# A PixArt block on one core: setup in single words and a new prelude order, gate-bias products on GpSimd, tokens in pairs, the query's cut ahead of the norms

## The chip, the cores and the metric

The kernel runs on one core of a Trainium2 chip. A core has four compute engines with instruction streams of their own: TensorE (PE; its weight loads are a second row, PEld), VectorE (DVE), ScalarE (ACT) and GpSimd (POOL). SyncE (SP) here only issues DMAs; ACT and POOL issue a few as well. The metric is the device time of one execution in microseconds (us); lower is better.

## The reference

A diffusion-transformer block over x of 16 batches x 256 tokens x 256 features, in float32, with 16 heads of 16 and a context of 256 tokens for each batch:

```
c_proj = silu(c) @ W_mod + b_mod          # shift_a, scale_a, gate_a, shift_m, scale_m, gate_m
x_norm = ln(x) * (1 + scale_a) + shift_a
q, k, v = split(x_norm @ W_qkv + b_qkv)
x = x + gate_a * (softmax(q k^T / 4) v @ W_proj + b_proj)
q_c = ln(x) @ W_qc + b_qc;  k_c, v_c = split(ln(context) @ W_kvc + b_kvc)
x = x + softmax(q_c k_c^T / 4) v_c @ W_cproj + b_cproj
x_norm2 = ln(x) * (1 + scale_m) + shift_m
x = x + gate_m * (gelu(x_norm2 @ W_mlp1 + b_mlp1) @ W_mlp2 + b_mlp2)
```

## The kernel before

Each operand of the large products is cut into a high and a low part of a reduced 32-bit type (`...h`, `...l` in tile names), and three products, high x high, high x low, low x high, make up one.

*Units.* An attention of one batch is a unit. There are 32: self-attention units s0 to s4, then s5 c0 s6 c1 ... s15 c10, then the cross-attentions c11 to c15. The MLP of all batches follows (the last 220 us of the span). A unit goes through eight beats. In each beat TensorE does the scores of the next unit (row maxima: score tiles `s` and `st`, maxima `mx` on DVE), the second scores `t` and exponentials of the current one, and pieces of what later units need. The table PLAN gives, for each of the eight beats, the words done ahead, the words of two lanes of TensorE (the two halves of the array's rows) and the words done after. `beat` turns each word into calls; units up to four ahead are being prepared while unit n runs.

*Order.* `InOrder` (L40-53) keeps every engine's instructions in the order in which the Python program issues them. So the words decide what stands behind what on each engine. All instructions carry line L51 in the profile, that helper's; they are told apart by tile names.

*Norms and cuts.* `layernorm` (L286) has three steps: the statistics on DVE, `rstd` (DVE aggregates, POOL adds epsilon and takes the power -0.5 in `rs`), and `apply`, on POOL in steady state (tile `xn_s` for x, `xn_c` for the context, `xn_q` for the cross-attention's query). `transposed` (L354) then turns xn on TensorE into `psT_...`, evacuates on ACT (`y_q`) and cuts on POOL: a copy to the high part (`xTh_q`), a subtraction for the low part (`xTl_q`). The query product `ps_qc` reads both. In PLAN's beat 6 the words `s6` and `e6` do rstd and apply of a unit four ahead; beat 7 ends in `Uc`, the cut of the query's transposed input of a unit three ahead.

*Keys and queries.* `to_stack` makes K and Q of a unit: product, high part on ACT (`h_k`, `h_q`), low part on DVE (`l_k`, `l_q`), and six DMAs of 128 KB for each of the two (`send`; words x, y for the high part, l for the low part, each 0 and 1) into a stacked buffer `big`, from which the scores are multiplied. A unit's first score matmul needs all twelve sends of its buffer.

*Prelude.* The string 'PRE' in `E_` (L55) is a list of words done in order before the first beat; 'SL' gives words done after beat k of unit n, as (n, k); n = -1 stands for the eight beats in which only unit 0's first scores run. `b12`, `b4` and so on are fillers: so many matmuls of a zero tile `wz` (`busy`, L155). `load` issues the loads of x of batch 0 (on ACT), the bias rows `brow` and the first weights. `brow` turns the bias rows into `bT`, `turn` turns silu(c) into `sT`, `scale` and `shift` are the two modulation products (both into `cpT`; `sc1` adds one to the scale, tile `sc`), `bk`, `bq`, `bv` are the bias products of the shift with the weights, `hik`/`lok` the cut of a weight (`hiv`/`lov` that of V, its low part on DVE). L, T, K, Q, V with a unit's number are norm, transposition, key, query and value: `L0a`, `L0b` statistics and rstd, `L0d` apply on DVE, `T0t` transposition, `T0h`/`T0l` high and low part; `K0a`, `K0m` the two halves of the key product, `K0h`, `K0l` its parts, `K0x0` ... `K0l1` its sends (with p: issued by POOL). `z0kp` zeroes a buffer on POOL, `M0` transposes maxima, `wm` loads the second modulation's weights, `ld3` loads a unit's input.

*The rest of the setup.* `setup_rest` (L211) is a generator; each word `rest` runs its next piece: the loads, then the attention's gate (`ps_ga`), the projected bias (`ps_pb`) and its product with the gate on DVE, then the cross-attention's bias (`ps_cb`), three weight loads and five cuts of weights. `f_gm` (L268) does the same for the MLP's gate: `ps_gm`, an addition and the product `gB` x gate, both on DVE, and a store to `gd`, from which each batch's gates are later read back.

Of the kernel before, what the change touches and what calls it, by code (L numbers as in the profile page):

```python
# [21 lines left out]
def pixart_block(  # L22
# [8 lines left out]
    B, N, H = x.shape  # L31
# [4 lines left out]
    KC = H // P  # L36
# [58 lines left out]
    BMOD, BQKV, BQC, BKVC, BM1 = 0, 12, 18, 20, 24  # L95
# [40 lines left out]
    st = psum.tile([P, 2, 512], F32, tag="st", name="st", bufs=1)  # L136
    sp = [psum.tile([P, 512], F32, tag=f"s{r}", name=f"s{r}", bufs=1) for r in range(2)]
# [73 lines left out]
    def setup_rest():  # L211
        gb = work.tile([B, 2, 2, H], F32, tag="pt", name="gb", bufs=5)
        gA, bb = gb[:, 0], gb[:, 1]
        bc = const.tile([1, H], F32, name="bc")
        wg, wp = stage(W_mod, 2 * H, "wga", "g", 3), stage(W_proj, 0, "wp_f", "g", 3)
        SP.dma_start(bb[:, 0], b_mod[2 * H:3 * H].partition_broadcast(B))
        SP.dma_start(bb[:, 1], b_proj.partition_broadcast(B))
        SP.dma_start(bc, b_cproj.partition_broadcast(1))
        wcp = stage(W_cproj, 0, "wcp_f", "x1", 7)
        yield  # L220
        pst = ps_gen("ps_ga")
        for k in range(KC):
            PE.matmul(pst[:B, :H], sT[:, k], wg[:, k], start=(k == 0), stop=(k == KC - 1))
        DVE.tensor_tensor(gA[:, 0], pst[:B, :H], bb[:, 0], ALU.add)
        yield
        pst = ps_gen("ps_pb")
        for k in range(KC):
            PE.matmul(pst[:B, :H], bqkv[:, 4 + k], wp[:, k], start=(k == 0), stop=(k == KC - 1))
# [3 lines left out]
        yield  # L232
        pst = ps_gen("ps_cb")
        for k in range(KC):
            PE.matmul(pst[:1, :H], bT[:, BKVC + 2 + k:BKVC + 3 + k], wcp[:, k],
                      start=(k == 0), stop=(k == KC - 1))
        DVE.tensor_tensor(bc, pst[:1, :H], bc, ALU.add)
        SP.dma_start(cd, bc)
        yield
        wkc, wqc = stage(W_kvc, 0, "wkc_f", "g", 3), stage(W_qc, 0, "wqc_f", "c", 2)  # L240
        wvc = stage(W_kvc, H, "wvc_f", "x1", 7)
        yield
        split(Wp[0], Wp[1], wp)
        yield
        split(Wkc[0], Wkc[1], wkc)
        yield
        split(Wqc[0], Wqc[1], wqc)
        yield
        split(Wvc[0], Wvc[1], wvc)
        yield  # L250
        split(Wcp[0], Wcp[1], wcp)

    wm = []

# [8 lines left out]
    gm = []  # L266

    def f_gm():  # L268
        w, gB = gm
        pst = ps_gen("ps_gm")  # L270
        for k in range(KC):
            PE.matmul(pst[:B, :H], sT[:, k], w[:, k], start=(k == 0), stop=(k == KC - 1))
        DVE.tensor_tensor(gB[:, 0], pst[:B, :H], gB[:, 0], ALU.add)
        DVE.tensor_tensor(gB[:, 1], gB[:, 1], gB[:, 0], ALU.mult)
        SP.dma_start(gd[:, 2:4], gB)

    def f_mods():
# [673 lines left out]
        build_pre(u)  # L951
        build_post(u)
    at = defaultdict(list)
    rest = setup_rest()

    u0, u1 = units[:2]
    def one_rows(i):
# [3 lines left out]
    u2 = units[2]  # L961
    word = {}
# [45 lines left out]
    word["rest"] = lambda: next(rest, None)  # L1008
    word["vone"] = lambda: [POOL.memset(v[:, :, :, HD:], 1.0) for v in vts]
    for n, f in (("load", f_load), ("silu", f_silu), ("turn", f_turn), ("brow", f_brow),  # L1010
                 ("scale", f_scale), ("sc1", f_sc1), ("shift", f_shift),
                 ("wm", f_wm), ("mods", f_mods), ("sc2", f_sc2), ("gm", f_gm)):
        word[n] = f
    for i in range(3):
# [8 lines left out]
    for i in range(3):  # L1023
        b = i if i < 2 else 0
# [26 lines left out]
    def visit(n, k, home=sp):  # L1051
# [22 lines left out]
    ]  # L1074
    lanes = {}

    def beat(n, k):
        if n < 0:
            s, t = visit(n, k, (st, sp)[k % 2])
# [19 lines left out]
        def attention(v, hf):  # L1099
# [4 lines left out]
        on = lambda v, f: f if v else lambda: None  # L1104
        T1 = lx and (lx.T[1],)
# [60 lines left out]
        s, t = visit(n, k, home)  # L1166
# [15 lines left out]
    last, o, q = units[-1], units[-1].post, units[-2].post  # L1182
# [86 lines left out]
```

## Time and profile before

| | us |
|---|---|
| median of 3 runs | 747.45 |
| lowest and highest of them | 747.15, 747.74 |
| profiled execution, its own time | 747.02 |
| its span, first to last instruction | 745.2 |

The clock granted to TensorE was 0.999 of full speed in the mean. A row of the timeline reads: start in us from the span's start, duration in us, engine, line, operation, tile written <- tiles read, partitions x elements and type of each, how many instructions the row stands for, and in brackets how long the engine had stood idle and whose end released it. PEld rows are weight loads, one for each matmul, overlapped with the matmul before. SPq, ACTq and POOLq rows are DMA issues. A row of instruction groups has three durations: least, median and largest in ns. A row of the windows view gives a stretch, its length, and for PE, PEld, DVE, ACT and POOL the busy time with the number of instructions, then the clock, the DMA engines' busy share and GB/s.

### The profile page before, as it was taken

Reading aid. Unit: us, or ns where it says so; the run is one execution under the profiler, and the core shown is the slowest. Engines: PE = TensorE matmul, PEld = TensorE weight load, DVE = VectorE, ACT = ScalarE, POOL = GpSimd, SP = SyncE. Lnnn points to the kernel's source line nnn. Section 1 sums busy time; section 2 is a strip of 40 time slices with the busy share of each in tenths; the row PEclk is TensorE's granted clock in tenths of the full one; section 3 lists DMA queues with packets and bytes.
Section 4 is the critical chain, followed back from the end, with each engine's and each line's share of the span. In section 5 each row is a group of like instructions: output and inputs, shape, how many; then the busy total and the mean of one; then the engine's idle time right before and its main releaser. Section 6 shows DMA issues by size and latency. Waiting matters only on the chain.

```text
span 745.2 us, 25296 instructions
## 1 busy us (share of the span) xinstructions
PE 736.1 (99%) x10144; PEld 649.2 (87%) x10144; DVE 575.2 (77%) x1188; ACT 564.1 (76%) x979; POOL 538.3 (72%) x569
## 2 busy tenths in 40 slices
PE   9999999999999999999999999999999999999997
PEld 8778888888888888888888888888879999999997
DVE  4888888888888888888888888888726656667662
ACT  4268898888888888888888887898886666666663
POOL 6757688869687696968769798798647666666652
PEclk9999999999999999999999999999999999999999
DMA  6754454543545445354545445455212132131320
GB/s 203 203 146 138 126 142 136 138 128 91 159 122 139 135 137 143 92 164 120 143 131 152 145 129 159 121 151 151 62 58 91 60 78 67 63 86 43 85 55 32
DMA packets 89049, 87.98 MB, mean 118 GB/s; under 512 B 8610, under 2 KB 84676, under 8 KB 88932
## 3 DMA queue, kind: packets, MB, share of 16 engines
q1 hardware_dynamic: 88468, 85.58, 40.8%
q8 instruction: 80, 1.31, 0.8%
q0 software_dynamic: 192, 0.52, 0.3%
q14 instruction: 37, 0.30, 0.1%
q10 hardware_dynamic: 272, 0.26, 0.1%
HBM read 26.97 MB, written 8.46 MB: 48 GB/s over the span
## 4 chain that ended last, share of the span: by engine, by line
PE 92%; POOL 4%; DVE 1%; issue 1%; DMA 1%; ACT 1%; POOLq 0%; DVEq 0%; ACTq 0%
PE s L51 17%; PE st L51 16%; PE o L51 15%; PE ph L51 11%; PE ps_qc L51 5%; PE ps_q L51 4%; PE ps_kc L51 3%; PE ps_P_s L51 3%; PE ps_k L51 3%; PE ps_v_c L51 3%; PE ps_v_s L51 2%; PE ps_P_c L51 2%; PE psT_q L51 1%; PE psA_s L51 1%; PE ps_h L51 1%; PE psT_m L51 1%
## 5 line engine op out<-in xcount | busy, mean ns | idle before, releaser
L51 DVE TENSOR_REDUCE mx<-s 128x2 f32<-128x512 f32 x504 | 324.6, 683 | 67.2 <-PE s L51 60.4
L51 ACT ACTIVATE pt<-st 128x1024 f32<-128x1024 f32 x252 | 258.9, 1027 | 17.0 <-PE st L51 11.6
L51 PE MATMUL s<-big 63*128 63x256 f32 (+1 forms) x1024 | 182.9, 297 | 0.7 <-DVE mx L51 0.6
L51 PEld LDWEIGHTS s<-big 63*128 63x128 f32 (+1 forms) x1024 | 132.8, 185 | 19.3 <-DVE l_kc L51 6.6
L51 PE MATMUL st<-big 64*128 64x256 f32 (+1 forms) x1024 | 134.1, 299 | 0.3 <-ACT pt L51 0.2
L51 POOL TENSOR_TENSOR hl<-hf,hh 128x512 fp32r<-128x512 f32 x64 | 84.7, 1326 | 64.8 <-ACT hh L51 64.7
L51 PE MATMUL o<-pt,v 128*32 128x256 f32 x2048 | 123.8, 382 | 0.0
L51 PEld LDWEIGHTS st<-big 64*128 64x128 f32 (+1 forms) x1024 | 95.3, 185 | 16.5 <-issue 12.9
L51 PEld LDWEIGHTS o<-pt,v 128*32 128x32 f32 x2048 | 60.0, 109 | 41.4
L51 ACT ACTIVATE hf<-ph,bT 128x256 f32<-128x256 f32 x114 | 47.8, 473 | 27.6 <-PE ph L51 27.6
L51 ACT ACTIVATE hh<-ph,bT 128x256 fp32r<-128x256 f32 x114 | 47.8, 471 | 22.5 <-PE st L51 11.8
L51 ACT COPY oT<-o 128x512 f32<-128x512 f32 x63 | 36.9, 586 | 33.0 <-PE o L51 33.0
L51 DVE TENSOR_SCALAR xn_m<-x,mv_m,rs_m 128x256 f32<-128x256 f32 x28 | 24.0, 901 | 32.4 <-POOL rs_m L51 32.4
L51 PE MATMUL s<-big,hh 128*128 128x256 f32 x256 | 46.7, 281 | 0.0
L51 PE MATMUL st<-big,hh 128*128 128x256 f32 x256 | 46.7, 281 | 0.0
L51 PE MATMUL ph<-wkch,wself 128*128 128x256 f32 x224 | 44.9, 284 | 0.0
L51 PE MATMUL ph<-wqch,wself 128*128 128x256 f32 x224 | 44.7, 284 | 0.0
L51 PE MATMUL ps_k<-xTh_s,wself 64*128 64x256 f32 (+1 forms) x232 | 43.9, 295 | 0.0
L51 PE MATMUL ps_q<-xTh_s,wself 64*128 64x256 f32 (+1 forms) x240 | 39.8, 283 | 0.4 <-DVE l_q L51 0.4
L51 POOL TENSOR_SCALAR xn_c<-c,mv_c,rs_c 128x256 f32<-128x256 f32 x32 | 39.0, 1227 | 1.7
L51 PE MATMUL ps_v_s<-wself,xTh_s 64*128 64x256 f32 x224 | 39.1, 294 | 0.0
L51 PE MATMUL ps_P_s<-wself,xTh_as 64*128 64x256 f32 x256 | 39.0, 282 | 0.0
(244 smaller groups left out, 2519.5 us busy)
## 6 DMA issues: line engine op xcount, KB each, us to landing
big<-h_kc SPq DMA_DIRECT2D x64, 128.0 KB
big<-h_qc SPq DMA_DIRECT2D x64, 128.0 KB
big<-h_k SPq DMA_DIRECT2D x62, 128.0 KB
big<-h_q SPq DMA_DIRECT2D x62, 128.0 KB
big<-l_k SPq DMA_DIRECT2D x32, 128.0 KB
big<-l_q SPq DMA_DIRECT2D x32, 128.0 KB
g<-gd SPq DMA_DIRECT2D x16, 256.0 KB
c<-in_ctx_dram SPq DMA_DIRECT2D x16, 256.0 KB
```

Source lines behind the costliest of these rows:

```text
L51: i = f(*a, **k)
```

## The change

`setup_rest` is split into single words: `lg`, `lp`, `lc`, `lx` for the loads, `ga`, `pb`, `cb` for the three products, `gs` for the product of gate and bias with the store, `sp0` to `sp4` for the cuts. The two products of gate and bias go from DVE to POOL. The tokens of x, context, the spill and the output are laid on partitions in pairs, so each partition holds 2 KB in one piece where it had two of 1 KB. `s6`/`e6` keep rstd alone; a new `s7`/`e7` after `Uc` does apply. PRE and SL have a new order, with other numbers of fillers:

```diff
-'PRE': 'z0qp z0kp load rest ld2 one0 silu b12 brow L0a turn L0b b4 L0d scale T0t sc1 hik lok L1a T0h L1b T0l b4 shift hiq K0a L1d bk loq K0m K0h K0x0 K0x1 K0y0p K0y1p T1t K0l T1h K0l0 K0l1 bq T1l Q0a Q0m Q0h Q0x0 Q0y0p Q0x1 Q0y1p Q0l Q0l0 Q0l1 z1kp z1qp K1a K1b hiv lov Q1a Q1b K1x0 K1x1 K1y0 K1y1 K1l K1l0 K1l1 Q1x0 Q1x1 Q1y0 Q1y1 Q1l Q1l0 Q1l1 L2a L2b L2c V0a V0b bv b9 ld3',
-'SL': {(-1, 0): 'V1a', (-1, 1): 'T2t T2h T2p vone z2kp z2qp', (-1, 2): 'V1b', (-1, 3): 'rest wm', (-1, 4): 'M0 rest one1 ld4', (-1, 5): 'K2a L3a', (-1, 6): 'K2m L3b L3p L3c', (-1, 7): 'mods sc2 one2 rest', (0, 0): 'gm rest', (0, 1): 'rest', (0, 4): 'rest', (0, 6): 'rest', (1, 0): 'rest', (1, 5): 'rest'}
+'PRE': 'b1 b4 load z0kp silu z0qp brow L0a L0b turn scale hik hiq ld2 sc1 L0d T0t T0h lok b3 loq shift T0l L1a L1b L2a hiv lg Q0a bk K0a lp one0 K0m bq lc L1d K0h K0y0p K0x1 Q0m K0l T1t K0l1 Q0h T1h lov T1l bv K1a K1b K0x0 K0y1p z1qp Q0y0p V0a Q1a Q0l Q0x0 K0l0 Q1b Q0l0 z1kp Q0l1 Q0y1p L2b V0b Q0x1 wm Q1l K1y0 Q1x1 K1l b6 ld3',
+'SL': {(-1, 0): 'Q1x0 L2c K1x0', (-1, 1): 'T2t K1l0 V1a T2h vone Q1l1 T2p', (-1, 2): 'V1b', (-1, 3): 'Q1y0 Q1y1 K1y1 pb K1x1 Q1l0 z2kp', (-1, 4): 'one1 L3a z2qp K1l1 ga', (-1, 5): 'K2a L3b K2m', (-1, 6): 'M0 gs', (-1, 7): 'ld4 mods L3p gm', (0, 0): 'L3c lx cb', (0, 4): 'one2', (0, 5): 'sp0', (0, 7): 'sp3 sc2 sp1', (1, 2): 'sp2', (1, 3): 'sp4'}
...
     def tok(ap, b):
-        return ap[b].rearrange("(t p) h -> p t h", p=P)
+        return ap[b].rearrange("(p t) h -> p t h", p=P)
...
+    def f_ga():
         pst = ps_gen("ps_ga")
         for k in range(KC):
-            PE.matmul(pst[:B, :H], sT[:, k], wg[:, k], start=(k == 0), stop=(k == KC - 1))
-        DVE.tensor_tensor(gA[:, 0], pst[:B, :H], bb[:, 0], ALU.add)
-        yield
+            PE.matmul(pst[:B, :H], sT[:, k], gA[2][:, k], start=(k == 0), stop=(k == KC - 1))
+        DVE.tensor_tensor(gA[0][:, 0], pst[:B, :H], gA[1][:, 0], ALU.add)
...
-        DVE.tensor_tensor(gA[:, 1], pst[:B, :H], bb[:, 1], ALU.add)
-        DVE.tensor_tensor(gA[:, 1], gA[:, 1], gA[:, 0], ALU.mult)
-        SP.dma_start(gd[:, 0:2], gA)
-        yield
+        DVE.tensor_tensor(gA[0][:, 1], pst[:B, :H], gA[1][:, 1], ALU.add)
+
+    def f_gs():
+        POOL.tensor_tensor(gA[0][:, 1], gA[0][:, 1], gA[0][:, 0], ALU.mult)
+        SP.dma_start(gd[:, 0:2], gA[0])
...
         DVE.tensor_tensor(gB[:, 0], pst[:B, :H], gB[:, 0], ALU.add)
-        DVE.tensor_tensor(gB[:, 1], gB[:, 1], gB[:, 0], ALU.mult)
+        POOL.tensor_tensor(gB[:, 1], gB[:, 1], gB[:, 0], ALU.mult)
         SP.dma_start(gd[:, 2:4], gB)
...
-        ("", "s t P12", "K2 t s K1 K9", "E n0 Uc"),
+        ("", "s t P12", "K2 t s K1 K9", "E n0 Uc s7 e7"),
...
-            "s6": on(ls, lambda: [f() for f in ls.ln[0].steps[1:]]),
+            "s6": on(ls, lambda: ls.ln[0].steps[1]()),
+            "s7": on(ls, lambda: ls.ln[0].steps[2]()),
             "e5": on(early, lambda: early.ln[1].steps[0]()),
-            "e6": on(early, lambda: [f() for f in early.ln[1].steps[1:]]),
+            "e6": on(early, lambda: early.ln[1].steps[1]()),
+            "e7": on(early, lambda: early.ln[1].steps[2]()),
```

The number of TensorE's instructions falls by the fillers left out (at the start, before the shift product and at the end of the prelude); in all other work only the order differs.

More of the change, by code (lines that the diff above doesn't have):

```diff
@@ new lines, in pixart_block @@
+    E_ = {'CUT': 8, 'LN': {'s': 'pool', 'c': 'pool', 'q': 'pool'}, 'ON': (1, 1, 1), 'L0': -16, 'L1': 1, 'S0': -7, 'A0': 0, 'T0': 1, 'S1': 5, 'A1': 7, 'L2': 9, 'T1': 9, 'S2': 32, 'AP': 23, 'DV': (0, 1), 'HP': (1, 0), 'BZ': {}, 'AV': {1: [(1, 2), (1, 3)], 9: [(0, 0), (0, 1)]}, 'AHEAD': (0, 0, 0, 0, 0, 2), 'TW': {(21, 6): 'cb', (23, 5): 'u0', (23, 7): 'u1', (25, 2): 'u2', (27, 3): 'u3', (27, 7): 'h2a', (28, 0): 'l2 h0p u5', (28, 2): 'h1p', (28, 4): 'h3p', (28, 7): 'u4 u6', (29, 0): 'l3d', (29, 1): 'l0', (29, 2): 'l1', (29, 7): 'h5p', (30, 1): 'u7 h6d h7p', (30, 3): 'h4p', (31, 1): 'l4 l6d', (31, 2): 'l5d x2', (31, 4): 'l7', (31, 7): 'b2'}, 'BE': 'G0 av P g0 A1 G1 G2 N1 F7 g1 S0 PF s2 G3 aT aL p2 a2 G4 x3 b3 S1 S2 T2 C r0 G5 S3 G6 S4 s3 CF x4 F8 g2 G7 S5 F9 p3 S6 G8 a3 r1 G9 F10 G10 T3 g3 b4 S7 s4 F11 S8 S9 F12 G11 p4 a4 F13 r2 S10 G12 x5', 'XP': 1, 'IL': 1, 'MF': 0, 'SH': 4, 'RAMP': 1, 'HA': 1, 'MP': 16, 'W': (7, 1, 0, 0), 'PRE': 'b1 b4 load z0kp silu z0qp brow L0a L0b turn scale hik hiq ld2 sc1 L0d T0t T0h lok b3 loq shift T0l L1a L1b L2a hiv lg Q0a bk K0a lp one0 K0m bq lc L1d K0h K0y0p K0x1 Q0m K0l T1t K0l1 Q0h T1h lov T1l bv K1a K1b K0x0 K0y1p z1qp Q0y0p V0a Q1a Q0l Q0x0 K0l0 Q1b Q0l0 z1kp Q0l1 Q0y1p L2b V0b Q0x1 wm Q1l K1y0 Q1x1 K1l b6 ld3', 'SL': {(-1, 0): 'Q1x0 L2c K1x0', (-1, 1): 'T2t K1l0 V1a T2h vone Q1l1 T2p', (-1, 2): 'V1b', (-1, 3): 'Q1y0 Q1y1 K1y1 pb K1x1 Q1l0 z2kp', (-1, 4): 'one1 L3a z2qp K1l1 ga', (-1, 5): 'K2a L3b K2m', (-1, 6): 'M0 gs', (-1, 7): 'ld4 mods L3p gm', (0, 0): 'L3c lx cb', (0, 4): 'one2', (0, 5): 'sp0', (0, 7): 'sp3 sc2 sp1', (1, 2): 'sp2', (1, 3): 'sp4'}}
@@ L221, in setup_rest, with f_loads_p, f_loads_c @@
+    def f_loads_p():
+        gA.append(stage(W_proj, 0, "wp_f", "g", 3))
+        SP.dma_start(gA[1][:, 1], b_proj.partition_broadcast(B))
+    cB = []
+    def f_loads_c():
+        cB.extend([const.tile([1, H], F32, name="bc"), stage(W_cproj, 0, "wcp_f", "x1", 7)])
+        SP.dma_start(cB[0], b_cproj.partition_broadcast(1))
+    def f_ga():
         pst = ps_gen("ps_ga")
         for k in range(KC):
[L223 removed]
@@ L224, in setup_rest, with f_pb @@
-        DVE.tensor_tensor(gA[:, 0], pst[:B, :H], bb[:, 0], ALU.add)
-        yield
+            PE.matmul(pst[:B, :H], sT[:, k], gA[2][:, k], start=(k == 0), stop=(k == KC - 1))
+        DVE.tensor_tensor(gA[0][:, 0], pst[:B, :H], gA[1][:, 0], ALU.add)
+    def f_pb():
         pst = ps_gen("ps_pb")
         for k in range(KC):
-            PE.matmul(pst[:B, :H], bqkv[:, 4 + k], wp[:, k], start=(k == 0), stop=(k == KC - 1))
-        DVE.tensor_tensor(gA[:, 1], pst[:B, :H], bb[:, 1], ALU.add)
-        DVE.tensor_tensor(gA[:, 1], gA[:, 1], gA[:, 0], ALU.mult)
@@ L231, in setup_rest, with f_cb @@
-        SP.dma_start(gd[:, 0:2], gA)
-        yield
+            PE.matmul(pst[:B, :H], bqkv[:, 4 + k], gA[3][:, k], start=(k == 0), stop=(k == KC - 1))
+        DVE.tensor_tensor(gA[0][:, 1], pst[:B, :H], gA[1][:, 1], ALU.add)
+    def f_gs():
+        POOL.tensor_tensor(gA[0][:, 1], gA[0][:, 1], gA[0][:, 0], ALU.mult)
+        SP.dma_start(gd[:, 0:2], gA[0])
+    def f_cb():
         pst = ps_gen("ps_cb")
         for k in range(KC):
-            PE.matmul(pst[:1, :H], bT[:, BKVC + 2 + k:BKVC + 3 + k], wcp[:, k],
+            PE.matmul(pst[:1, :H], bT[:, BKVC + 2 + k:BKVC + 3 + k], cB[1][:, k],
@@ L251, in setup_rest, with f_loads_x, f_split @@
-        split(Wcp[0], Wcp[1], wcp)
+        DVE.tensor_tensor(cB[0], pst[:1, :H], cB[0], ALU.add)
+        SP.dma_start(cd, cB[0])
+    def f_loads_x():
+        cB.extend([stage(W_kvc, 0, "wkc_f", "g", 3), stage(W_qc, 0, "wqc_f", "c", 2),
+                   stage(W_kvc, H, "wvc_f", "x1", 7)])
+    def f_split(i):
+        w = (Wp, Wkc, Wqc, Wvc, Wcp)[i]
+        split(w[0], w[1], (gA, cB, cB, cB, cB)[i][(3, 2, 3, 4, 1)[i]])
     wm = []
@@ L1007, in pixart_block @@
     word["M0"] = lambda: m_part(u0, 0)
-    word["rest"] = lambda: next(rest, None)
+    for i in range(5):
+        word[f"sp{i}"] = lambda i=i: f_split(i)
     word["vone"] = lambda: [POOL.memset(v[:, :, :, HD:], 1.0) for v in vts]
```

30 lines of the change are left out of this document (6 added, 24 removed).

## The prediction

> **What bounds the kernel now.** I read the profile's page first: the busy times and the chain that ended last.
>
> ```profile
> span 745.2 us, 25296 instructions
> PE 736.1 (99%) x10144; PEld 649.2 (87%) x10144; DVE 575.2 (77%) x1188; ACT 564.1 (76%) x979; POOL 538.3 (72%) x569
> PE 92%; POOL 4%; DVE 1%; issue 1%; DMA 1%; ACT 1%; POOLq 0%; DVEq 0%; ACTq 0%
> ```
>
> TensorE works 99% of the span and no other engine passes 77%. So an edit is worth something only where TensorE waits, or works slowly. The next view is the timeline of a steady stretch (unit c3), engine by engine, around the query of the cross-attention.
>
> ```profile
> 165.82 0.59 ACT L51 COPY y_q<-psT_q 128x512 f32<-128x512 f32 x1
> ...
> 167.28 2.43 POOL L51 TENSOR_SCALAR xn_s<-x,mv_s,rs_s 128x256 f32<-128x256 f32 x2
> ...
> 169.66 0.61 POOL L51 CAST xTh_q<-y_q 128x512 fp32r<-128x512 f32 x1
> ...
> 170.35 1.29 POOL L51 TENSOR_TENSOR xTl_q<-y_q,xTh_q 128x512 fp32r<-128x512 f32 x1
> ...
> 171.38 0.27 PE L51 MATMUL ps_qc<-xTh_q,wqch 64*128 64x256 f32 x1
> 171.50 0.27 PE L51 MATMUL ps_qc<-xTh_q,wqcl 64*128 64x256 f32 x1
> ...
> 171.70 0.39 PE L51 MATMUL ps_qc<-xTl_q,wqch 64*128 64x256 f32 x1
> 171.93 0.28 PE L51 MATMUL ps_qc<-xTl_q,wqch 64*128 64x256 f32 x1
> ```
>
> ACT hands over y_q at 166.41, but POOL is about to do the norm xn_s (2.43 us), which stands ahead of the query's cut in program order. The low part xTl_q ends at 171.64; 0.06 later the first matmul that reads it issues. Matmuls of this row issue every 0.12 us (171.38 to 171.50). Here the steps are 0.20 and 0.23, so TensorE loses 0.08 + 0.11 = 0.19 us. No wait is printed, since the loss is below what the view lists; the duration 0.39 instead of 0.28 is the mark of it. Two units show it larger, with the wait printed:
>
> ```profile
> 447.38 0.28 PE L51 MATMUL ps_qc<-xTh_q,wqcl 64*128 64x256 f32 x1
> 447.81 0.39 PE L51 MATMUL ps_qc<-xTl_q,wqch 64*128 64x256 f32 x1 [0.15 <-POOL xTl_q L51]
> ...
> 513.03 0.28 PE L51 MATMUL ps_qc<-xTh_q,wqcl 64*128 64x256 f32 x1
> 513.51 0.39 PE L51 MATMUL ps_qc<-xTl_q,wqch 64*128 64x256 f32 x1 [0.20 <-POOL xTl_q L51]
> ```
>
> By the same count these lose 0.43 - 0.12 + 0.11 = 0.42 and 0.48 - 0.12 + 0.11 = 0.47. The 0.39 mark stands in 14 of the 16 units; the group of all 128 has it as its maximum, with 278 ns as the median:
>
> ```profile
> L51 PE MATMUL ps_qc<-xTl_q,wqch x128: 273/278/392, 106.9 to 517.1; 64*128 64x256 f32 x128
> ```
>
> The last stretch read is the prelude, to the first score matmul at 24.27.
>
> ```profile
> 0.72 0.45 ACTq L51 DMA_DIRECT2D x<-in_x_dram  x1
> ...
> 1.04 5.19 PEld L51 LDWEIGHTS s<-wz 128*128 128x128 f32 x24 [1.04 <-DVE wz L51]
> ...
> 1.65 0.47 SPq L51 DMA_DIRECT2D brow<-in_bias_rows_dram  x1
> ...
> 3.64 0.75 DVE L51 BATCH_NORM_STATS2 st_s<-x 128x6 f32<-128x256 f32 x2
> ...
> 6.46 0.31 PE L51 MATMUL s<-ident,brow 32*128 32x32 f32 x1
> 6.48 0.73 DVE L51 TENSOR_SCALAR xn_s<-x,mv_s,rs_s 128x256 f32<-128x256 f32 x2 [1.87 <-POOL rs_s L51]
> ...
> 6.81 0.18 ACT L51 COPY bT<-s 128x32 f32<-128x32 f32 x1 [3.68 <-PE s L51]
> 6.89 1.00 PEld L51 LDWEIGHTS s<-wz 128*128 128x128 f32 x8
> ...
> 7.81 0.97 PEld L51 LDWEIGHTS st<-sT,wf 128*128 128x128 f32 x8
> ...
> 8.99 0.19 DVE L51 TENSOR_TENSOR cpT<-st,bT 128x32 f32<-128x32 f32 x1 [1.77 <-PE st L51]
> ...
> 10.37 0.88 DVE L51 SCALAR_TENSOR_TENSOR xTl_s<-psT_s,sc,xTh_s 128x256 fp32r<-128x256 f32 x2
> ...
> 15.17 0.18 DVE L51 TENSOR_TENSOR bqkv<-st,bT 128x32 f32<-128x32 f32 x1
> ...
> 17.12 0.88 DVE L51 SCALAR_TENSOR_TENSOR l_q<-ps_q,bqkv,h_q 128x256 fp32r<-128x256 f32 x2 [0.99 <-ACT h_q L51]
> ...
> 18.93 1.19 SPq L51 DMA_DIRECT2D big<-l_q  x2
> 19.10 0.69 DVE L51 TENSOR_TENSOR wself<-wf,wself 128x512 fp32r<-128x512 f32 x1 [1.10 <-ACT wself L51]
> ...
> 24.27 0.83 PE L51 MATMUL st<-big 63*128 63x256 f32 x4
> ```
>
> The fillers on zeros show two speeds of TensorE: 24 loads in 5.19 us are 0.216 each, the next 8 take 1.00, 0.125 each, and the 8 of the scale product 0.97, 0.121 each. The array became fast only after some 5.5 us of work without a break from 1.04 on.
>
> **The change part by part.** *Query ahead of norms* (s7, e7). POOL does the two query operations before xn_s, so xTl_q ends 2.43 us earlier, about 169.2, and TensorE finds it ready at 171.50. Gain: 12 x 0.19 + 0.42 + 0.47 = 3.17 us if every loss goes; as neighbouring losses can pass on to the next wait I take 2.7, with 1.6 (half) and 3.2 as ends. What is late next is xn_s: it now ends where xTl_q did, 171.64. Who reads it is shown by the chain of waits:
>
> ```profile
> 172.98 0.06 PE psT_s L51
> ```
>
> That leaves some 1.3 us, less in units where TensorE takes psT_s sooner; this is the cover. Without it each unit would lose up to 2.43 less 1.3, 1.1 us.
>
> *Prelude order.* It removes fillers. A filler is two loads (b12 is the row of 24, b4 that of 8). Ahead of the scale product stood b12 and b4, now b1 and b4 in one go; ahead of the shift product b4, now b3; at the end b9, now b6. So the first fillers are 10 loads, done at 1.04 + 10 x 0.216 = 3.2; then TensorE waits for brow. brow is issued at 1.65; x, issued at 0.72, was used at 3.64, 2.9 later, so I take 4.55. Transposition and copies: bT was copied 0.35 after its transposition began; sT follows; the scale product starts at 5.4. Its 8 loads are now slow, 1.73, not 0.97: end 7.15, cpT 7.35, the factor 7.6. Program order on DVE now puts the first norm behind it: xn_s 7.75 to 8.48 (before 6.48 to 7.21). From 8.2 TensorE transposes (4 loads), runs the filler (6) and the shift product (8): 18 x 0.216 = 3.9, to 12.1. xTl_s, which needs the shift, then runs 12.6 to 13.5 where it ran 10.37 to 11.25: 2.2 later. That unbroken stretch from 8.2 would, by the 5.5 us that the row of fillers shows, turn the array fast at 13.7, so what follows goes at its old durations. The chain of waits has one for a product of 12 loads:
>
> ```profile
> 14.71 1.50 PE ps_q L51 x12
> ```
>
> After the cut, TensorE ends the first half of Q0's product (13.8), the key bias (8 loads, 0.97), K0 (1.50) and the query bias (0.97): 17.2, and bq is added at 17.4 (before 15.17).
>
> Weighing a page: the Trainium skill, "TensorE: Matmul & The Clock Gate", Part 1, says the array starts at half rate and is let up to full rate by a window of about 3.4 us of sustained work, the windows running freely. By that, an estimate, the turn would come between 11.6 and 15.0, and the sum would move by about -0.7 to +0.6 us; the trace agrees so far that its 5.5 us lie between one such window and two.
>
> DVE then does in order xn_s of batch 1 (0.73), l_k (0.88), the value weights' low part (0.69), xTl_s of batch 1 (0.88), the value bias (0.18) and l_q (0.88): 17.4 + 4.24 = 21.65, where l_q ended at 18.0. l_q's two sends are the last that the first score waits for; the second started at 19.5 (half of the 1.19 from 18.93), and now at 22.7, pushed by SP's other issues. It landed at most 24.27 - 19.5 = 4.8 later. In that stretch the DMA engines were nearly full:
>
> ```profile
> 8.00:24.40 16.40, 15.96 (x136) 15.44 (x135) 9.92 (x29) 6.52 (x15) 10.09 (x13) 1.00 0.78 213
> ```
>
> 78% of their time over the 16.4 us. Three us later less stands ahead, as unit 1's sends and three 256 KB loads come behind, so I take 3.7: first score at 26.4 (bounds 25.8 with 3.1, 27.5 with 4.8). Before, its four matmuls held TensorE 0.83 for the usual 0.50, so 24.27 + 0.33 = 24.6 is the point to compare. Prelude: +1.8 us (1.2 to 2.9). TensorE's own work is no tighter: K1 can't start before the cut of batch 1's transposed input, 20.6, and K1, V0, Q1 and the last 12 loads of filler end at 25.7 by 0.125 a load.
>
> *First units.* Here TensorE waits before:
>
> ```profile
> 26.87 0.31 PEld L51 LDWEIGHTS psT_s<-ident,xn_s 128*128 128x128 f32 x3 [0.36 <-POOL xn_s L51]
> ...
> 40.78 1.06 DVE L51 TENSOR_TENSOR gB<-gB 16x256 f32<-16x256 f32 x1
> ...
> 42.49 0.18 PEld L51 LDWEIGHTS s<-big 63*128 63x128 f32 x1 [0.54 <-DVE mx L51]
> 43.09 0.29 PEld L51 LDWEIGHTS s<-big 63*128 63x128 f32 x3 [0.42 <-DVE mx L51]
> ```
>
> The first goes because L2a (batch 2's statistics) and its norm come earlier against the scores. The other two follow the 1.06 us product gB x gate on DVE, just ahead of the row maxima that TensorE needs; it moves to POOL, where nothing waits for it but its own store. Gain 0.36 + 0.54 + 0.42 = 1.32; ends 0.4 (a wait returns elsewhere, POOL being busier) and 1.7. The product gA x gate moves likewise. The gate and bias matmuls are the same in number and only change places (cb and gm swap units): nothing, as TensorE is full in both. Covered by POOL's slack, 28% of the span.
>
> *Token pairs.* x, context, the spill and the output are moved as 2 KB a partition, not 2 x 1 KB. No transfer of these ends a wait in steady state; taken as nothing. If it does change, half the packets of 256 KB loads frees DMA time, a gain; a loss would need a wait on these loads, and none is printed: 0 to -0.3.
>
> Sum: 1.8 - 1.32 - 2.7 = -2.2. The profiled execution took 747.02 (its span 745.2 and 1.8 around it), so 744.8; the median of the runs is 747.45, 0.43 above it, so 745.2. Own range: best 1.2 - 1.7 - 3.2 = -3.7, worst 2.9 - 0.4 - 1.6 = +0.9; the ends won't meet, so 743.9 to 746.6.
>
> **The rivals.** (a) *The array turns fast early*: it needs only work in a sum or a fixed time after the start, not an unbroken 5.5 us, so it is fast near 6.9 as before. For: the row gives just one turn, so both readings fit. Against: the gap from 3.2 to 4.55. Then scale ends 6.4, shift about 10, and the first score comes at 23.5, a gain of 1.1 where the forecast has a loss of 1.8: 745.2 - 2.9 = 742.3, and with the later parts a little worse, 742.4 to 742.7.
> (b) *The query's stall is only passed on*: TensorE arrives sooner at the next score matmuls and waits there for DVE's maxima or POOL's xn_s. For: margin 1.3 against 2.43 moved. Against: DVE at 77%. Gain 0 to 0.2, sum 1.8 - 1.3 + 0 = +0.4: 747.8.
> (c) *A later prelude*: the turn at 15 and the longest landing, first score 27.7: 1.2 to 1.4 more, 746.3 to 746.6.
> (d) *Slower*: in the new order TensorE meets a short wait before each stretch of 5.5 us is full (for brow, for the factor, for the first norm, for xTl_s), and the array stays slow up to the first score. Place: the prelude; it decides if the stretch from 8.2 breaks before 13.7. Then the products of bk, K0, bq, Q0, the value bias, K1, Q1 and V0, some 84 loads on the path, take 0.095 each more, 8.0: near 753. Against: shift, K0 and both bias products queue without a wait on another engine except the cut of xTl_s.
>
> **How the numbers follow.** Chances: forecast 0.49, (a) 0.15, (b) 0.12, (c) 0.12, (d) 0.12. From this kernel's spread of runs 0.2%, 1.5 us, is about what can be told from no change: faster is below 745.95, slower above 748.95. Of the forecast 0.42 lies below 745.95 and 0.07 above; with (a) faster 0.57, same 0.07 + (b) + (c) = 0.31, slower (d) 0.12. Predicted 745.2; the range 742.4 to 747.8 leaves out (d) and little else.
>
> **What would show it.** Right: the second filler row and the scale's loads at 0.21 each, a first score near 26.4; ps_qc's low matmuls all at 0.28 with xTl_q ending 2.4 earlier against its unit; no wait on mx after the gB product; psT_s not waiting for xn_s. Wrong: loads at 0.12 before 8 us (a), ps_qc still at 0.39 or as much wait at the next scores (b), first score past 28 (c, d), or waits for m or x in the first two units, which I cost at nothing.

## The result, and the profile after

The changed kernel takes 758.69 us (median of 5 runs, 756.33 to 760.25), the kernel before 747.34 (5 runs, 746.57 to 747.74). The ratio is 1.0148, with a 95% interval of 1.0132 to 1.0164: 11 us slower, where 2 us faster was forecast. The profiled execution took 758.97, its span 757.2.

The page of the kernel after, its span, busy times and the chain that ended last:

```profile
span 757.2 us, 25222 instructions
PE 739.2 (98%) x10114; PEld 652.9 (86%) x10114; DVE 578.6 (76%) x1186; ACT 564.4 (75%) x979; POOL 539.5 (71%) x571
PE 93%; DVE 2%; POOL 1%; DMA 1%; ACT 1%; issue 1%; SPq 0%; POOLq 0%; ACTq 0%; DVEq 0%
```

TensorE is still the bound, and it is busy 3 us longer with 30 instructions fewer: some of them must run slower. Where, the timeline of the prelude shows (all engines, start and duration in us):

```profile
1.04 2.21 PEld L51 LDWEIGHTS s<-wz 128*128 128x128 f32 x10 [1.04 <-DVE wz L51]
...
7.59 1.24 DVE L51 TENSOR_SCALAR sc<-cpT 128x32 f32<-128x32 f32 x1
...
8.75 1.68 DVE L51 TENSOR_SCALAR xn_s<-x,mv_s,rs_s 128x256 f32<-128x256 f32 x2
8.96 1.31 POOL L51 TENSOR_TENSOR wself<-wf,wself 128x512 fp32r<-128x512 f32 x1 [0.17 <-ACT wself L51]
...
15.88 1.82 PEld L51 LDWEIGHTS st<-cpT,wf 128*128 128x128 f32 x8
...
20.15 1.82 PEld L51 LDWEIGHTS st<-cpT,wf 128*128 128x128 f32 x8
...
22.12 0.19 DVE L51 TENSOR_TENSOR bqkv<-st,bT 128x32 f32<-128x32 f32 x1 [4.08 <-PE st L51]
22.23 5.12 DVE L51 TENSOR_SCALAR xn_s<-x,mv_s,rs_s 128x256 f32<-128x256 f32 x2
...
22.70 1.82 POOL L51 MEMSET big<- 128x2048 f32 x1
...
24.97 1.82 POOL L51 MEMSET big<- 128x2048 f32 x1
...
27.00 0.18 PEld L51 LDWEIGHTS psT_s<-ident,xn_s 128*128 128x128 f32 x1 [3.74 <-DVE xn_s L51]
...
30.11 0.86 DVE L51 SCALAR_TENSOR_TENSOR l_q<-ps_q,bqkv,h_q 128x256 fp32r<-128x256 f32 x2
...
36.70 0.50 PE L51 MATMUL st<-big 63*128 63x256 f32 x4
```

Two things are to be seen. The bias products at 15.88 and 20.15 still take 1.82 for 8 loads, the slow 0.22 each: the array has not turned fast at 13.7. And DVE's norm of batch 1 at 22.23 takes 5.12 us for what took 0.73 in the quiet row of before; POOL does two clearings of a buffer meanwhile, and TensorE's loads stand for 3.74 us, its matmuls for 3.45. The clock column of the windows view does not show the slow array here:

```profile
16.00:24.00 8.00, 7.55 (x36) 7.25 (x35) 2.78 (x6) 1.25 (x4) 3.54 (x5) 1.00 0.15 42
```

It reads 1.00 while the loads take 0.22. Ahead of the first turn one has to go by the loads.

Further on, the query's wait is gone as forecast. The timeline of the same unit as before (c3), and the group of all 128 matmuls:

```profile
180.79 1.28 POOL L51 TENSOR_TENSOR xTl_q<-y_q,xTh_q 128x512 fp32r<-128x512 f32 x1
182.05 2.44 POOL L51 TENSOR_SCALAR xn_s<-x,mv_s,rs_s 128x256 f32<-128x256 f32 x2
...
184.60 0.28 PE L51 MATMUL ps_qc<-xTl_q,wqch 64*128 64x256 f32 x1
...
185.45 0.14 PEld L51 LDWEIGHTS psT_s<-ident,xn_s 64*128 64x128 f32 x1
```

```profile
L51 PE MATMUL ps_qc<-xTl_q,wqch x128: 272/277/283, 120.1 to 527.3; 64*128 64x256 f32 x128
```

xTl_q is done 2.5 us before its first reader, xn_s ends 1.0 us before its reader, and the maximum of the group is 283 ns, not 392.

The times of the first score and of the first and the last of these matmuls give an account of the span, after less before:

| stretch, up to | before | after | difference so far | of this stretch | forecast |
|---|---|---|---|---|---|
| first score | 24.27 | 36.70 | +12.4 | +12.4 | +2.1 |
| first ps_qc low | 106.9 | 120.1 | +13.2 | +0.8 | -1.6 |
| last ps_qc low | 517.1 | 527.3 | +10.2 | -3.0 | -2.7 |
| end of the span | 745.2 | 757.2 | +12.0 | +1.8 | 0 |

(The forecast's 0.33 for the first score's own length is counted in the second line here.) The loss is the prelude, with 1.8 more at the end; the steady state does what was forecast. In the second stretch TensorE has a new wait. Timeline of the kernel after near 64 us:

```profile
60.65 0.25 ACT L51 ACTIVATE m<-psm 16x128 fp32r<-16x128 f32 x1
...
61.49 1.19 SPq L51 DMA_DIRECT2D big<-l_q  x2
...
62.73 1.45 SPq L51 DMA_DIRECT2D big<-ones  x2
...
64.27 0.55 SPq L51 DMA_DIRECT2D big<-m  x1
...
66.20 0.35 PE L51 MATMUL st<-big 64*128 64x256 f32 x1 [1.37 <-DMA big<-m]
```

ACT has m ready at 60.90, SP issues it at 64.27, behind the two sends of ones for unit 2 that the new order put at (0, 4). The windows view shows what follows that wait (columns as before; the clock is the number behind the five busy times):

```profile
64.00:66.00 2.00, 0.83 (x9) 0.66 (x7) 1.04 (x4) 1.23 (x3) 1.90 (x3) 1.00 0.08 22
66.00:68.00 2.00, 1.79 (x20) 1.14 (x24) 1.37 (x3) 0.76 (x2) 1.91 (x3) 0.64 0.37 126
68.00:70.50 2.50, 2.50 (x30) 1.04 (x24) 0.71 (x2) 0.56 (x2) 2.42 (x3) 0.60 0.33 80
70.50:74.00 3.50, 3.50 (x55) 3.50 (x55) 2.53 (x4) 2.57 (x4) 1.42 (x2) 1.00 0.62 166
```

After 2 us in which TensorE is busy for 0.83, the granted clock falls: of these 4.5 us some 3.4 were at half rate (2.00 x 0.36 / 0.5 + 2.50 x 0.40 / 0.5), then it comes back. TensorE does 50 matmuls in these 4.5 us, and 55 in the 3.5 behind them; by that count, an estimate, the slow stretch costs 1.3 us, and a wait of 1.4 us about twice its own length.

### The profile page after: what moved, and what is told of

It reads as the page before. It is cut to its first block, busy times and chain, and to the rows that moved or that the text cites. A ratio compares the mean times of both kernels' runs of the same rounds, so it can differ in the third digit from the quotient of the medians.

```text
span 757.2 us, 25222 instructions
## 1 busy us (share of the span) xinstructions
PE 739.2 (98%) x10114; PEld 652.9 (86%) x10114; DVE 578.6 (76%) x1186; ACT 564.4 (75%) x979; POOL 539.5 (71%) x571
## 4 chain that ended last, share of the span: by engine, by line
PE 93%; DVE 2%; POOL 1%; DMA 1%; ACT 1%; issue 1%; SPq 0%; POOLq 0%; ACTq 0%; DVEq 0%
PE st L51 17%; PE s L51 16%; PE o L51 16%; PE ph L51 11%; PE ps_q L51 5%; PE ps_qc L51 4%; PE ps_v_c L51 3%; PE ps_kc L51 3%; PE ps_k L51 3%; PE ps_P_s L51 3%; PE ps_v_s L51 2%; PE ps_P_c L51 2%; PE psT_q L51 1%; PE psA_s L51 1%; PE psT_m L51 1%; PE ps_h L51 1%
## 5 line engine op out<-in xcount | busy, mean ns | idle before, releaser
L51 PE MATMUL ps_k<-xTh_s,wself 64*128 64x256 f32 (+1 forms) x232 | 45.9, 304 | 0.0
```

What stands on the lines that cost most here:

```text
L51: i = f(*a, **k)
```

## The experiments

Theory C: the array is slow through the prelude, since the granted rate depends on how full a stretch of a few us was. Theory P: DVE's norms can't run while POOL works. The rivals stand in the expectations. All medians below are compared with runs of the kernel before on the same chip.

**The query's cut alone.** On the kernel before:

```diff
-        ("", "s t P12", "K2 t s K1 K9", "E n0 Uc"),
+        ("", "s t P12", "K2 t s K1 K9", "E n0 Uc s7 e7"),
...
-            "s6": on(ls, lambda: [f() for f in ls.ln[0].steps[1:]]),
+            "s6": on(ls, lambda: ls.ln[0].steps[1]()),
+            "s7": on(ls, lambda: ls.ln[0].steps[2]()),
...
-            "e6": on(early, lambda: [f() for f in early.ln[1].steps[1:]]),
+            "e6": on(early, lambda: early.ln[1].steps[1]()),
+            "e7": on(early, lambda: early.ln[1].steps[2]()),
```

> The kernel before, with only the query's cut moved ahead of the norms (s7, e7 after Uc). Theory 1 (POOL's xn ahead of the cut costs TensorE 0.19 us in each of 12 units, 0.42 and 0.47 in two): 747.3 - 2.8 = 744.5 us, ps_qc's low matmuls all at 0.28. Rival (the stall is passed on to the next wait): 746.8 to 747.3. Xn_s later by 1.9 us has 1.3 us of cover: if that is too little, psT_s waits and the time is over 747.3.

744.11 against 747.43 (ratio 0.9953, interval 0.9940 to 0.9967), 3.3 us less. All low matmuls take 272 to 279 ns, and the stretch from the first to the last of them is 407.1 us, where before has 517.1 - 106.9 = 410.2. This part of the prediction holds, and nothing passes the wait on.

**Fillers back.** On the kernel after, in PRE:

```diff
-b1 b4 load ... L0a L0b turn scale ... lok b3 loq shift
+b12 load ... L0a L0b turn b4 scale ... lok b4 loq shift
```

> The changed kernel with the fillers of before up to the shift product (b12 at the start, b4 ahead of the scale product, b4 ahead of the shift product); the rest of the order stays new. Theory C (the slow array from 7 to 32.5 us is most of the 12.1 us by which the first score is later): array fast near 7, first score 36.7 - 7.5 = about 29, time about 751. Theory P (the norm of batch 1 on DVE, 5.12 us while POOL clears a buffer and issues DMAs, is most of it): the norm still takes about 5, first score 34 or later, time 756 or more.

756.88 (4 runs; ratio 1.0123, 1.0104 to 1.0142). This is the time that P expected, not C's 751: the norm of batch 1 still takes 5.12, and the first score comes at 37.1. It is no failure of C all the same, as the windows of this run show:

```profile
4.00:10.70 6.70, 4.70 (x40) 4.27 (x40) 3.01 (x9) 1.83 (x5) 4.81 (x5) 1.00 0.94 310
10.80:34.50 23.70, 19.98 (x92) 19.16 (x91) 11.19 (x23) 4.32 (x11) 10.87 (x14) 0.50 0.33 94
34.70:48.00 13.30, 13.30 (x105) 10.39 (x103) 11.92 (x22) 4.54 (x11) 6.93 (x8) 1.00 0.62 170
```

The array did turn fast, and lost the rate again at 10.7, after TensorE had stood 2.0 us in two waits (7.5 to 9.8) for the factor and the norm of batch 0, whose second half here ran beside POOL's weight cut. Then it stayed slow for 24 us. C took the turn for a single event; it can be undone.

**The clearings ahead.** On the kernel after:

```diff
-lok b3 loq shift ... K0y1p z1qp Q0y0p ... Q0l0 z1kp Q0l1
+lok b3 loq z1qp z1kp shift ... K0y1p Q0y0p ... Q0l0 Q0l1
```

> The changed kernel with the two clearings of unit 1's buffer (z1qp, z1kp) moved ahead to where POOL stands idle (behind loq), so that they no longer run beside the norm of batch 1. Theory P: that norm falls from 5.12 to 0.7 to 1.7 us, TensorE's break of 3.45 us before psT_s goes, first score about 32.5, time about 754.5. Theory C: the array is still slow when that norm comes, the most that can go is the break, and the array turns fast at the earliest after the bias product of the values; time 754 to 756. If the norm's length has another cause than POOL's clearing, it stays near 5 us and the time near 758.7.

753.63, with a wide spread (750.44 to 758.04; ratio 1.0084, 1.0056 to 1.0112). In the timeline of the profiled run both norms are short, and the first score comes at 31.5:

```profile
8.09 0.73 DVE L51 TENSOR_SCALAR xn_s<-x,mv_s,rs_s 128x256 f32<-128x256 f32 x2
...
20.62 0.73 DVE L51 TENSOR_SCALAR xn_s<-x,mv_s,rs_s 128x256 f32<-128x256 f32 x2
```

The norm of batch 0 is short without an edit to it, since POOL's second weight cut starts only at 8.97 here. That of batch 1 has lost the clearings beside it, but not all work of POOL:

```profile
19.77 1.36 POOL L51 DMA_DIRECT2D big<-h_k  x2 [4.20 <-ACT h_k L51]
```

So P is right as to the clearings: without them the norm of batch 1 takes 0.73, not 5.12, and POOL's DMA issues alone did not hold it. But this run also tells against the rule of the prediction, since TensorE's weight loads are still slow long after 8.6, with no break over 0.57 us between:

```profile
18.54 1.82 PEld L51 LDWEIGHTS st<-cpT,wf 128*128 128x128 f32 x8
```

They become fast near 27.6, among the products of V0.

**Both.** On the kernel after:

```diff
-b1 b4 load ... L0a L0b turn scale ... lok b3 loq shift ... K0y1p z1qp Q0y0p ... Q0l0 z1kp Q0l1
+b12 load ... L0a L0b turn b4 scale ... lok b4 loq z1qp z1kp shift ... K0y1p Q0y0p ... Q0l0 Q0l1
```

> The changed kernel with both edits: the fillers of before up to the shift product, and the two clearings ahead. If C and P together hold all of the prelude's loss: first score near 26, time about 748 (the first units' wait for the maxima m and the store at the end still cost). If a third cause is left in the new order, the first score stays past 28 and the time past 750.

757.10 (4 runs; ratio 1.0133, 1.0119 to 1.0146) and a first score at 37.1, a miss. The clearings now met the norm of batch 0; timeline:

```profile
8.85 5.26 DVE L51 TENSOR_SCALAR xn_s<-x,mv_s,rs_s 128x256 f32<-128x256 f32 x2
8.90 1.26 POOL L51 TENSOR_TENSOR wself<-wf,wself 128x512 fp32r<-128x512 f32 x1 [0.28 <-ACT wself L51]
...
10.10 3.55 POOL L51 MEMSET big<- 128x2048 f32 x2
...
13.85 0.82 PEld L51 LDWEIGHTS psT_s<-ident,xn_s 128*128 128x128 f32 x4 [5.53 <-DVE xn_s L51]
```

The norm ends 0.5 us behind the third instruction of POOL in a row, and its first reader starts only at 13.85: no part of it was done between them. The 5.5 us break took the array's rate with it. This is P seen a second time, at another norm.

**Fillers, and the norm of batch 0 where it was.** On the kernel after, fillers as above, and:

```diff
-L0a L0b turn b4 scale hik hiq ld2 sc1 L0d T0t
+L0a L0b turn b4 L0d scale hik hiq ld2 sc1 T0t
```

> The changed kernel with the fillers of before up to the shift product and the norm of batch 0 back ahead of the scale product (L0d before sc1); the norm of batch 1 stays beside the clearings. Theory C+P (the array's rate is granted from window to window; the breaks that DVE's norms make while POOL works take it back): the array turns fast near 4 to 7 and passes the stretch to 11, where the kernel with fillers alone lost it; the norm of batch 1 still takes about 5 us and breaks TensorE for 3, so first score near 29, and time 748 to 750, or up to 755 where that break costs the rate again. Rival (fillers and norms are side matters, the new order of weights and sends is the loss): first score past 33, time over 754.

751.52 (4 runs; ratio 1.0059, 1.0045 to 1.0073), in the upper part of what C+P expected. The first score, at 33.3, is later than C+P's 29 and just past the rival's 33, whose time of over 754 did not come. In the windows view the rate comes and goes:

```profile
13.40:16.60 3.20, 3.20 (x16) 3.20 (x17) 0.24 (x2) 0.46 (x2) 0.62 (x1) 0.50 0.02 5
16.80:20.00 3.20, 1.26 (x10) 1.05 (x10) 2.71 (x2) 1.02 (x3) 3.07 (x4) 1.00 0.44 123
20.20:30.20 10.00, 7.66 (x35) 7.44 (x36) 5.98 (x12) 1.68 (x4) 5.83 (x7) 0.50 0.49 130
```

The first slow stretch begins behind the shift and key-bias products, where TensorE's only break was 0.50. The norm of batch 1 (from 17.40, 5.50 us) then empties the stretch before 20.2, and 10 slow us follow.

**All three steps undone.** Also the norm of batch 1 ahead of the key bias:

```diff
-Q0a bk K0a ... bq lc L1d K0h
+Q0a L1d bk K0a ... bq lc K0h
```

> The changed kernel with three steps undone: the fillers up to the shift product, the norm of batch 0 ahead of the scale product, and the norm of batch 1 ahead of the key bias (L1d before bk), where POOL has no clearing to do. C+P: array fast from 4 to 7 on and never slow again before the first score, which comes at 24 to 25.5; time 747.4 + 0.5 - 1 - 2.9 = 744, up to 747 where the wait for the maxima m at the first t scores (1.4 us, and 2 for a slow window after it) comes again. Rival as for the run before: first score past 28.

744.73 (10 runs, 743.51 to 748.47; ratio 0.9975, 0.9960 to 0.9991): 14 us below the kernel after, and below the kernel before. The profiled run has its first score at 24.0 and a norm of 0.74. So the fillers and the two norms hold the prelude's loss: of the 14 us, 12.7 lie ahead of the first score. What is left of the new order stands 0.6 above the kernel with all parts but the order (744.10, below), less than the spread of either. The wait for m is still there (1.2 us ahead of the loads of the first t scores).

**Narrow fillers.** On the kernel before:

```diff
-            PE.matmul(where[:, :P], wz, wz, start=True, stop=True)
+            PE.matmul(where[:, :16], wz, wz[:, :16], start=True, stop=True)
```

> The kernel before with its fillers made 16 columns wide, not 128: as many weight loads, each as long, but an eighth of the columns streamed. If what turns the array fast is columns streamed in a window, and products of 16 columns hardly count: no turn near 7, loads at 0.21 past 10 us, first score 4 to 9 us later, time 751 to 756. If any unbroken work counts: the turn at about 7 and the time 747.4 as before.

756.10 (4 runs; ratio 1.0123, 1.0095 to 1.0150): 9 us lost by the fillers' columns alone. The weight loads of the first 12 us in the timeline, then a window:

```profile
1.04 5.19 PEld L51 LDWEIGHTS s<-wz 128*128 128x128 f32 x24 [1.04 <-DVE wz L51]
...
6.70 1.78 PEld L51 LDWEIGHTS s<-wz 128*128 128x128 f32 x8
8.37 1.83 PEld L51 LDWEIGHTS st<-sT,wf 128*128 128x128 f32 x8
```

```profile
32.20:38.90 6.70, 6.70 (x32) 5.44 (x32) 3.47 (x4) 1.57 (x4) 2.22 (x3) 0.50 0.78 220
```

The first row is the same as before's, 24 loads in 5.19 us, without a break; the second is slow where before's ran at 0.125 a load. So it is not how long or how densely the loads run that turns the array fast; the columns that the fillers stream count, and the bias products of this kernel have 16. In the last filler, 18 loads of 16 columns ending near 33, the rate went again at 32.2. The first score of this run comes at 33.0.

**Wide fillers in the new order.** On the kernel after:

```diff
-lok b3 loq shift ... K0y1p z1qp Q0y0p ... Q0l0 z1kp Q0l1
+lok b16 loq z1qp z1kp shift ... K0y1p Q0y0p ... Q0l0 Q0l1
```

> The changed kernel with the clearings ahead, as in the run that first moved them, and 16 fillers (32 loads of 128 columns) ahead of the shift product, not 3. Theory C with columns: TensorE works without a break from about 9 on in both, and what kept the array slow to 27.7 there were the products of 16 columns in every window; 32 wide loads fill one window whole, so the array turns fast inside the fillers, between 13 and 17. The fillers cost 4 to 5.6 us, some 72 later loads save 0.095 each, 6.8: first score about 29.5 for 31.5, time about 2 us below that run, 751 to 752. Rival (the turn needs a long unbroken stretch, whatever its columns): still slow at 20, first score about 36, time 757 to 759.

754.06 (5 runs, 749.72 to 755.12; ratio 1.0085, 1.0057 to 1.0113). The mechanism came as expected, the time did not. In this run's timeline:

```profile
8.09 5.16 DVE L51 TENSOR_SCALAR xn_s<-x,mv_s,rs_s 128x256 f32<-128x256 f32 x2
...
13.78 4.84 PEld L51 LDWEIGHTS s<-wz 128*128 128x128 f32 x32
18.55 0.97 PEld L51 LDWEIGHTS st<-sT,wf 128*128 128x128 f32 x8
```

32 loads in 4.84 us, 0.15 each, are a mixture of slow and fast: the array turned within these fillers, and every product behind them is fast. But the clearings hit the norm of batch 0 again (5.16), so that the fillers began at 13.78, where those of the run with the clearings ahead began at 9.36, 4.4 us earlier; the first score came at 33.0.

**The sends of ones back.** On the kernel with all three steps undone:

```diff
-(-1, 7): 'ld4 mods L3p gm', (0, 0): 'L3c lx cb', (0, 4): 'one2', (0, 5): 'sp0'
+(-1, 7): 'ld4 mods L3p one2 gm', (0, 0): 'L3c lx cb', (0, 5): 'sp0'
```

> The changed kernel with the three steps undone as in the run before, and the two sends of ones for unit 2's buffer (one2) back in the stage ahead of unit 0, as in the kernel before. Theory: SP issues these two (1.45 us) between the maxima m's last step on ACT and m's send, and TensorE waits 1.2 us for m; without them m lands 1.5 us earlier and the wait is gone: 744.7 - 1.2 = 743.5, and, as the slow windows that sometimes follow that wait go too, all runs within 1.5 us of one another where they lay 5 apart. Rival (m waits for the full DMA queues): the wait stays, 744.7.

744.08 (6 runs, 742.33 to 748.68; ratio 0.9959, 0.9947 to 0.9972). In the profiled run m is sent right behind l_q, and TensorE doesn't wait for it:

```profile
55.55 1.18 SPq L51 DMA_DIRECT2D big<-l_q  x2
56.83 0.57 SPq L51 DMA_DIRECT2D big<-m  x1
```

The expected step is 1.2, the medians differ by 0.65, and the spreads of both kernels are wider than that, so the size isn't settled. That the spread would shrink was wrong. This profiled run is the slowest one, 748.68, and its windows say why:

```profile
7.00:13.70 6.70, 6.20 (x52) 5.91 (x53) 4.15 (x12) 2.67 (x6) 2.96 (x4) 1.00 0.69 239
13.80:27.30 13.50, 13.50 (x66) 13.50 (x65) 4.32 (x14) 3.35 (x8) 10.48 (x13) 0.50 0.55 153
```

The kernel with all three steps undone has the same order up to here, and its profiled run kept the rate; this one lost it at 13.7, with TensorE busy 6.20 of 6.70 us. The scale, shift and key-bias products of 16 columns fill 2.9 us of that stretch. The new order seems to stand near an edge; where it lies was not measured.

**Products on POOL, token pairs, and both with the query.** On the kernel before; first the query's cut (its diff above) with this:

```diff
-        DVE.tensor_tensor(gA[:, 1], gA[:, 1], gA[:, 0], ALU.mult)
+        POOL.tensor_tensor(gA[:, 1], gA[:, 1], gA[:, 0], ALU.mult)
...
-        DVE.tensor_tensor(gB[:, 1], gB[:, 1], gB[:, 0], ALU.mult)
+        POOL.tensor_tensor(gB[:, 1], gB[:, 1], gB[:, 0], ALU.mult)
```

> The kernel before with the query's cut ahead of the norms and the two products of gate and bias on POOL, nothing else. If the products' part is right (0.54 + 0.42 us of waits for DVE's maxima behind the gB product), it is 1.0 us below the run with the query's cut alone: 743.1. If POOL is too busy there or the wait is another's: 744.1.

743.13 (5 runs, 741.92 to 744.69; ratio 0.9951, 0.9937 to 0.9964), by the medians 1.0 below the query's cut alone. Against the runs of before beside each it is 4.0 for 3.3, and the spreads overlap, so the size of the step isn't settled. Another effect is as large: from 40 to 60 us the mean clock is 0.91 in the profiled run of the query's cut alone, 1.00 in this one, and 0.91 again in the run of all three edits below. The wait itself is gone. DVE goes from the addition straight to the next maxima:

```profile
39.30 0.40 DVE L51 TENSOR_TENSOR gB<-ps_gm,gB 16x256 f32<-16x256 f32 x1
39.64 1.27 DVE L51 TENSOR_REDUCE mx<-s 128x2 f32<-128x512 f32 x2
```

The pairs alone:

```diff
-        return ap[b].rearrange("(t p) h -> p t h", p=P)
+        return ap[b].rearrange("(p t) h -> p t h", p=P)
```

> The kernel before with only the tokens laid in pairs (2 KB packets). Forecast: nothing that can be told, 747.1 to 747.5. Rival (half the packets free DMA time in the crowded prelude): first score up to 0.5 us earlier, 746.6 to 747. Rival (longer packets end later, the last store above all): 0.5 to 1.3 us more.

746.88 (11 runs) against 746.87: ratio 1.0001, 0.9993 to 1.0010. The pairs are worth nothing.

And all three edits together:

> The kernel before with the query's cut ahead of the norms, the products on POOL and the token pairs: all of the change but the new order of the prelude. If the pairs are worth nothing: 743.1 as without them. This would be the best of all versions if the new order, with its three steps undone, gains nothing of its own.

744.10 (6 runs, 742.64 to 746.12; ratio 0.9963, 0.9952 to 0.9974). With the pairs or without, these lie within one another's spread. The lowest median is that of the query's cut with the products, 743.13: 15.6 us below the kernel after and 4.0 below the kernel before. The three versions with the query's cut can't be told from one another (their intervals overlap).

## Why the prediction was wrong

*The query.* Forecast -2.7, measured -3.0 in the profile and -3.3 alone. The 0.39 marks were read rightly, and the cover of xn_s held with 1.0 us left.

*The products.* Forecast 0.54 + 0.42. The mechanism is right: the loads' waits for mx from 26 to 62 us add up to 2.1 us in the kernel before and to 1.0 with the products on POOL. The size, 0.7 to 1.0 by the medians, agrees but is not clear of the spread.

*The pairs.* Forecast nothing, measured nothing.

*The step that failed* stands in the prelude: "That unbroken stretch from 8.2 would, by the 5.5 us that the row of fillers shows, turn the array fast at 13.7, so what follows goes at its old durations." The array turned near 32.4. Up to the factor the forecast had held (bias rows transposed at 4.61 for 4.55, the factor begun at 7.59 for 7.6). Three things were wrong in that sentence.

First, work was taken for work. The 5.5 us were fillers of 128 columns; of the stretch from 8.2, 8 loads are the shift product, and bk and bq follow, all with 16 columns. The narrow fillers show that such loads count for little: as long, as dense, and no turn. With 32 wide loads the array turned inside them, in the new order too. The rule in full is open. K0's twelve products of 256 columns, with a bias product on either side, turned the array in none of the six traces of the new order in which it was slow there. In the seven traces that turned late, the turn came 2.7 to 6.0 us behind the last product of 16 columns.

Second, the stretch was not unbroken, and the break was a mis-sized term. The norms of both batches were costed at 0.73, the quiet row. Two other rows of the timeline of before would have warned:

```profile
11.34 1.27 POOL L51 TENSOR_TENSOR wself<-wf,wself 128x512 fp32r<-128x512 f32 x1
...
11.41 1.67 DVE L51 TENSOR_SCALAR xn_s<-x,mv_s,rs_s 128x256 f32<-128x256 f32 x2
```

The same kind of norm takes 1.67 there, beside POOL's weight cut. The new order put the factor and both norms beside POOL's work: 1.24 for 0.18, 1.68 and 5.12 for 0.73. The last is the largest single term, 4.4 us, and made the longest break.

Third, the rate was taken as won for good. It is lost after a stretch with little streamed, as the runs with fillers show, and as the wait for m shows at 66. How much streaming keeps it was not measured.

How the first score came at 36.70 for the 26.4 of the forecast can be followed at DVE's rows, forecast against after: xTl_s of batch 0 from 12.6 to 14.33 (+1.7: the factor and the norm); the query's bias added from 17.4 to 22.12 (+3.0 more: two bias products, half of Q0 and K0 slow); the norm of batch 1 (+4.4); so l_q ends at 30.97 for 21.65. In the end the first score hung on TensorE, which from the late norm (27.00) on works without a break up to it, K1 still slow, and not on the landing of l_q on which the forecast's range rested.

*The rivals.* (d) named the right place and the right outcome, an array that stays slow up to the first score or nearly so, and priced it at 8 us and 753 with a chance of 0.12. Its reason, a short wait in each stretch, is half of it. What was held against it, that "shift, K0 and both bias products queue without a wait on another engine", is true in the trace (15 to 23.5 us) and did not help, for the reason given first. Its price lacked the norm's 4.4.

*The first units.* The forecast gain came (no wait on maxima behind gB, none for xn_s at the first scores), but the wait for m, costed at nothing ("Wrong: ... waits for m or x in the first two units"), took 1.37 and a slow window after it: +0.8 in all for the forecast -1.6.

*The end.* The last store ran from 752.29 to 757.2, 4.9 us, where before has 745.2 - 741.71 = 3.5. With the pairs alone it is 746.1 - 742.56 = 3.5 too. In the other traces of the new order it is 4.8 to 4.9 wherever the norm of batch 0 stands behind the scale product, and 3.7 to 3.8 in the three runs that put it ahead. Why is not known; so some 1.2 of the 14 us that the three steps give back lie at the end and not in the prelude.

The Trainium skill, "SBUF — State Buffer", section "Who interferes with whom", says that DVE's tensor_scalar can take a port pair that it shares with GpSimd, and that the one which comes second is blocked for the whole instruction. The runs agree that it blocks: 0.73 alone, 5.12 to 5.50 beside clearings. The section also says that the first to issue gets the pair, and here the rows differ. In the kernel after, the norm at 8.75 begins 0.21 ahead of POOL's cut, and its first half is read at 9.20: it went through. But the norm at 8.85 in the run with both edits, 0.05 ahead of POOL's, was held until POOL had finished three instructions, and that at 17.40 in the run with fillers and norm, 0.84 ahead of the clearing's row, until POOL had finished its clearings.

## What to carry to other kernels

A warm-up filler is judged by the columns it streams, not by how long or densely its loads run, and the work behind it must keep streaming: behind a chain of products with few columns, or one wait of 1.4 us, the rate went back here. A new order in which that happens only sometimes shows as a spread of 5 us over runs. Before an instruction of DVE is moved, look at what POOL does at the new place, and take the duration from the row of before where POOL was busy, not from the quiet one. Each part of a large change is worth trying alone: here the query's cut holds all of the gain that the runs can tell, and the new order of the prelude more than all of the loss.

## What the runs showed of the hardware

- A DVE tensor_scalar on float32 in SBUF (two of 128x256 in a row) takes 0.73 us with POOL idle, and 0.73 while POOL only issues DMAs; it takes 1.68 beside one cut of POOL's and 5.12 to 5.50 beside two clearings.
- The array's rate is granted and taken back many times: slow for 3.4 us after the wait for m, from 10.7 to 34.6 in another run, and fast, slow, fast, slow, fast within 31 us in a third. TensorE's busy share alone did not tell when: at 6.20 of 6.70 us busy with many 16-column products the rate was taken.
- Fillers of 24 loads with 16 columns run as long as 24 with 128 (5.19 us) while the array is slow, and did not make it fast.
